# Cross-attention block: Q, K, V and the output projection by seven blocks, softmax weights left undivided, and a new order of all engines

## The chip, the cores and the metric

One core of one Trainium2 chip. The metric is device time in microseconds (us) for one launch of the kernel; of several runs the median is given. The engines are PE (TensorE, with PEld its weight loads), DVE (VectorE), ACT (ScalarE), POOL (GpSimd) and SP (SyncE, which here only issues transfers).

## The reference

128 batches of 128 tokens of 256 features, all in float32. Queries come from `x`, keys and values from `ctx_1024`; there are 16 heads of 16 features, and a token may attend only to the tokens ahead of it.

```python
q = (query @ Wq + bq)...; k = (key @ Wk + bk)...; v = (values @ Wv + bv)...   # 16 heads of 16
scores = einsum('bhqd,bhkd->bhqk', q, k) / 4
scores = where(j < i, scores, -1e30)
attn = softmax(scores, axis=-1);  attn[:, :, 0, :] = 0
attn_out = einsum('bhqk,bhkd->bhqd', attn, v)... @ Wo + bo
x = layer_norm(query + attn_out, ln1_g, ln1_b)
out = layer_norm(x + (relu(x @ W1 + b1) @ W2 + b2), ln2_g, ln2_b)      # W1: 256 x 1024
```

## The kernel before, in words

Batches go in pairs: there are NP = 64 pairs, and a pair has TP = 256 tokens. `KC` = 2 counts the 128-wide halves of the 256 features, `FC` = 8 those of the 1024 hidden ones. Nothing schedules the work: each engine runs its instructions in the order in which the code issues them (a manual schedule), and waits by semaphores where it needs another engine.

After a start written out by hand (`third` to `sixth`), the function `step(p)` (L1475) runs for p = 7 to 63, and a tail follows. One step does one part each for several pairs: the scores, exponentials and turning of pair p; queries and keys of pair p + 1 and values of pair p; the weighing of the values, the output projection and the first norm's statistics of pair p - 2; the first feed-forward product of pair p - 3; the second of pair p - 4; the second norm and the store of pair p - 5.

PE in a step: `weigh` (L544, L554) multiplies the turned softmax weights `pT` with the values in blocks of 32 columns. `scores_both` (L410) fills banks 0 to 3 with the scores of each batch's later 64 queries ("high", 128 keys) and banks 4 to 7 with those of the earlier 64 ("low", 64 keys). Then come queries and keys (`project`, L270), the output projection (`attention_out`, L573) and the values (`values`, L325): each is four matmuls of 128 x 128 weights with 256 moving columns. The two feed-forward products (`second_by_seven`, L878, and `Hidden.run`, L990) already go by seven block products in place of eight: 28 matmuls of 128 columns each, over sums and differences of blocks that POOL makes (`combine_hidden`, L859 to L862, and `combine_normed`, L952 to L955, with `w1t` and `wt` made once). Between the matmuls of L878 stand empty PE instructions (L219). The seven products lie in banks of their own, and DVE adds them up from there (L903, L919 and L926; L1002 to L1016).

DVE masks the high scores in their banks (L820) and takes maxima (L823); the low scores go to SBUF with their mask (L426, L434) and then get their maximum (L829). ACT takes the exponentials head by head with the row sum as a second output (L839). POOL then divides the weights by the row sums (`inverse` and `divide`, L480 and L485: three instructions of 1024 elements). DVE turns them in 32 x 32 blocks (`turn`, L497), and 16 transfers within SBUF put the blocks in place (`bring`, L512). ACT copies the weighed values (`context`, L566, tile `cxT`), the queries (L296), the keys twice, each time with half of the features set to zero (L315), and the values in two layouts (L340 `vz`, L349 `vd`), and does the relu (L1021) and both norms' scaling (L625, L662). POOL also adds the output bias to `x` (L263), makes the norms' scale and shift (L593, L594, L648), the residual (L637, L640) and the second norm's gain and bias (L672, L676). The normed tokens are turned by DVE (L742) and go through DRAM by four writes and one read (L246, L251).

Softmax weights, the turned blocks and `pT` of all pairs share four wide buffers (`wide`).

## Time and profile before

| | before |
|---|---|
| runs | 1483.75, 1484.87, 1485.62 us; median 1484.87 us |
| profiled execution | span 1482.7 us from its first to its last instruction; its own time is not given apart, the median of the runs is 2.2 us more |
| busy share of the span | PE 99%, PEld 93%, DVE 93%, ACT 89%, POOL 93% |
| granted TensorE clock | 0.999 |
| DMA | 204.63 MB, mean 138 GB/s |

How to read it: a share of busy time says how full an engine is, not how long it is waited for. PE's matmuls overlap, so the time of one is read from start to start, or from a run of equal ones; the same holds for two neighbours on DVE or ACT, where the next one starts before the record of the last one ends. A row such as `707.05 0.42 DVE L820 ...` gives start, duration, engine, line and operation, then output and inputs with their shapes; in square brackets stands the idle time ahead of it, and who ended it.

### The profile page before, as it was taken

Reading aid. Unit: us, or ns where it says so; the run is one execution under the profiler, and the core shown is the slowest. Engines: PE = TensorE matmul, PEld = TensorE weight load, DVE = VectorE, ACT = ScalarE, POOL = GpSimd, SP = SyncE. Lnnn points to the kernel's source line nnn. Section 1 sums busy time; section 2 is a strip of 40 time slices with the busy share of each in tenths; the row PEclk is TensorE's granted clock in tenths of the full one; section 3 lists DMA queues with packets and bytes.
Section 4 is the critical chain, followed back from the end, with each engine's and each line's share of the span. In section 5 each row is a group of like instructions: output and inputs, shape, how many; then the busy total and the mean of one; then the engine's idle time right before and its main releaser. Section 6 shows DMA issues by size and latency. Waiting matters only on the chain.

```text
span 1482.7 us, 53916 instructions
## 1 busy us (share of the span) xinstructions
PE 1475.0 (99%) x19367; PEld 1378.1 (93%) x19367; DVE 1386.3 (93%) x2444; ACT 1324.1 (89%) x5272; POOL 1376.5 (93%) x1530
## 2 busy tenths in 40 slices
PE   9999999999999999999999999999999999999998
PEld 7788999999999999999999999999999999999998
DVE  7999999999999999999999999999999999999977
ACT  6668999999999999999999999999999999999963
POOL 6979999999999999999999999999999999999987
PEclk9999999999999999999999999999999999999999
DMA  8366666555655566665556556566655666555451
GB/s 201 79 133 150 148 150 141 127 146 138 154 144 133 138 146 138 149 144 130 144 132 156 146 128 143 144 137 150 145 132 141 136 153 148 128 141 131 109 137 51
DMA packets 415317, 204.63 MB, mean 138 GB/s; under 512 B 282448, under 2 KB 383056, under 8 KB 415056
## 3 DMA queue, kind: packets, MB, share of 16 engines
q1 hardware_dynamic: 412768, 199.34, 57.5%
q8 instruction: 160, 2.62, 0.8%
q10 hardware_dynamic: 2288, 1.85, 0.5%
q14 instruction: 101, 0.83, 0.2%
HBM read 70.26 MB, written 33.29 MB: 70 GB/s over the span
## 4 chain that ended last, share of the span: by engine, by line
PE 96%; DVE 2%; POOL 1%; ACT 0%; issue 0%; DMA 0%; POOLq 0%; DVEq 0%
PE banks L878 25%; PE banks L990 25%; PE banks L270 15%; PE banks L573 7%; PE banks L325 7%; PE banks L410 6%; PE banks L554 4%; PE banks L544 2%; PE banks L778 2%; PE banks L1042 0%; PE banks L797 0%; DVE su L468 0%; POOL sm L446 0%; PE banks L527 0%; POOL sm L470 0%
## 5 line engine op out<-in xcount | busy, mean ns | idle before, releaser
L839 ACT ACTIVATE sm<-banks,nmx 128x128 f32<-128x128 f32 x944 | 329.8, 377 | 16.3 <-DVE nmx L823 8.7
L485 POOL TENSOR_TENSOR sm<-sm,rs 128x1024 f32<-128x1024 f32 x171 | 322.6, 1901 | 0.0
L839 ACT ACTIVATE sm<-sm,nmx 128x64 f32<-128x64 f32 x944 | 312.5, 368 | 0.0
L497 DVE STREAM_TRANSPOSE tb<-sm 128x1024 f32<-128x1024 f32 x186 | 229.8, 1237 | 17.1 <-DMA pT<-tb 6.9
L1021 ACT ACTIVATE hT<-hT,b1e_c 128x256 f32<-128x256 f32 x464 | 198.1, 497 | 34.7 <-DVE hT L1009 21.0
L839 ACT ACTIVATION_READ_ACCUMULATOR sm<-sm,nmx 128x1 f32 x912 | 201.6, 221 | 0.0
L839 ACT ACTIVATION_READ_ACCUMULATOR sm<-banks,nmx 128x1 f32 x912 | 197.3, 216 | 0.0
L990 PE MATMUL banks<-xS,w1t 128*128 128x128 f32 x1392 | 174.4, 275 | 0.0
L878 PE MATMUL banks<-wt,hS 128*128 128x128 f32 x1440 | 170.7, 275 | 0.0
L878 PEld LDWEIGHTS banks<-wt,hS 128*128 128x128 f32 x1440 | 165.6, 192 | 0.1
L990 PEld LDWEIGHTS banks<-xS,w1t 128*128 128x128 f32 x1392 | 164.8, 192 | 0.0
L823 DVE TENSOR_REDUCE nmx<-banks 128x4 f32<-128x512 f32 x177 | 153.9, 869 | 6.0
L270 PE MATMUL banks<-xT,wq 128*128 128x256 f32 x504 | 125.4, 392 | 0.0
L315 ACT ACTIVATE kT<-banks,bkh,half 128x256 f32<-128x256 f32 x252 | 122.5, 590 | 2.8 <-PE banks L270 2.8
L990 PE MATMUL banks<-x1T,w 128*128 128x128 f32 x944 | 124.6, 275 | 0.2 <-DMA x1T<-x1t 0.2
L573 PE MATMUL banks<-wo,cxT 128*128 128x256 f32 x512 | 121.2, 379 | 0.0
L325 PE MATMUL banks<-wv,cT 128*128 128x256 f32 x512 | 121.0, 379 | 0.0
L270 PE MATMUL banks<-cT,wk 128*128 128x256 f32 x504 | 119.4, 380 | 0.1
L878 PEld LDWEIGHTS banks<-w,hT 128*128 128x128 f32 x944 | 114.7, 192 | 3.1
L990 PEld LDWEIGHTS banks<-x1T,w 128*128 128x128 f32 x944 | 114.9, 192 | 0.4 <-issue 0.3
L878 PE MATMUL banks<-w,hT 128*128 128x128 f32 x944 | 115.2, 275 | 0.0
L573 PEld LDWEIGHTS banks<-wo,cxT 128*128 128x128 f32 x512 | 97.0, 190 | 13.5 <-ACT cxT L566 0.3
(191 smaller groups left out, 3954.1 us busy)
## 6 DMA issues: line engine op xcount, KB each, us to landing
pT<-tb SPq DMA_DIRECT2D x976, 96.0 KB, 2.2
x1t<-tbx SPq DMA_DIRECT2D x252, 64.0 KB, 2.4
x1T<-x1t SPq DMA_DIRECT2D x63, 256.0 KB, 3.0
out_dram<-t SPq DMA_DIRECT2D x63, 256.0 KB, 3.1
xb<-in_x_dram SPq DMA_DIRECT2D x124, 128.0 KB, 3.7
cb<-in_ctx_dram SPq DMA_DIRECT2D x124, 128.0 KB, 4.2
x<-in_x_dram SPq DMA_DIRECT2D x31, 512.0 KB, 5.3
w<-in_L_xattn_W_dram SPq DMA_DIRECT2D x2, 1024.0 KB, 8.3
```

Of the source, the lines that this page charges most:

```text
L270: nc.tensor.matmul(ps[:, m * TP : (m + 1) * TP], w[:, k, m * P : (m + 1) * P], src[:, k, :], start=(k == 0), stop=(k == KC - 1),)
L315: nc.scalar.activation(st["kT"][:, m, e, :], pk[:, m * TP : (m + 1) * TP], AF.Identity, bias=bkh[:, m, e : e + 1], scale=half[:, e : e + 1],)
L325: nc.tensor.matmul(pv[:, s * D : (s + 1) * D], st["cT"][:, k, s * P : (s + 1) * P], wv[:, k, :], start=(k == 0), stop=(k == KC - 1),)
L410: nc.tensor.matmul(st["sps", hi][r][s * HP : (s + 1) * HP, m * 2 * n : (m + 1) * 2 * n].rearrange("p (e j) -> p e j", e=2), st["qT"][strip ...
L485: nc.gpsimd.tensor_tensor(sm[:, part, :], sm[:, part, :], st["rs", hi][:, part, None].to_broadcast([P, part.stop - part.start, sm.shape[2] ...
L497: nc.vector.transpose(st["tb"][:, :, at : at + 256].rearrange("p j (n a) -> p n j a", a=32), st["sm", hi].rearrange("p h j -> p (h j)")[:, ...
L573: nc.tensor.matmul(po[:, s * D : (s + 1) * D], cxT[:, k, s, :], wo[:, k, :], start=(k == 0), stop=(k == KC - 1),)
L823: nc.vector.tensor_reduce(st["nmx", 1][:, 4 * first : 4 * (first + n)], ps, AX.X, ALU.max, negate=True,)
L839: nc.scalar.activation(sm[:, h, :], src, AF.Exp, bias=nmx[:, h : h + 1], scale=1.0, **({"accum_out": st["su", hi][:, h : h + 1]} if summed ...
L878: nc.tensor.matmul(out, left(k), right(k), start=(k == 0), stop=(k == FC // 2 - 1))
L990: nc.tensor.matmul(ps[:, i * P : (i + 1) * P].rearrange("p (n a) -> p n a", a=32), left(i), right, start=True, stop=True,)
L1021: nc.scalar.activation(self.hT[:, f], self.plains.get(f, self.hT[:, f]), AF.Relu, bias=b1e_c[:, f : f + 1], scale=1.0,)
```

## The change

Four things change, from p = 7 on.

*Products.* Queries, keys, values and output projection go by seven block products too (class `Seven`). The seven are not kept apart: they run as chains that add up in three 128-column parts of one PSUM bank. Part 0 takes product 1, then 6, 7 and 4 on top; part 1 takes 2 alone; part 2 takes 5, then 3. After 1, after 6 and after 7 ACT or DVE takes what part 0 holds so far, and only then may PE add the next product; after 4 the last reader takes it. The second feed-forward product (`Second`) gets the same form, and so does the first (`First`, with three whole banks as its parts). POOL makes the sums of blocks of `xT`, `cT` and `cxT` (four instructions of 128 columns each), and once those of the four weights. ACT writes the keys once, and then spreads them into two halves, one by ACT and one by POOL. The empty PE instructions are gone from the steps.

*Undivided weights.* POOL's `divide` goes. DVE inverts the 32 row sums of a row at once and turns them (`inverse`); they go to DRAM and are read back spread over the partitions (`send_inverse`, `fetch_inverse`); DVE multiplies them in where ACT copied the weighed values (`context`).

*Transfers.* The 16 moves of `bring` become four writes to DRAM and one read (`send_weights`, `fetch_weights`); the read of pair p - 1 stands in the middle of step p. Softmax weights, turned blocks and `pT` have one buffer each in place of four shared ones. The inverses take four small writes and two reads.

*Order.* `step(p)` walks a list of 150-odd short names. Each stands for one small piece of work; a suffix -1 or -2 means that it belongs to a step one or two earlier. The last pair has a function of its own (`last_step`), in the old order.

```diff
+    def inverse(p):
+        rs = small.tile([P, 2 * H], F32, tag="rs", name=f"rs_{p}")
+        rt = st["rt"] = small.tile([P, 32], F32, tag="rt", name=f"rt_{p}")
+        nc.vector.reciprocal(rs, st.pop("su"))
+        nc.vector.transpose(rt, rs)
...
+    def fetch_inverse(p):
...
+            nc.sync.dma_start(
+                inv[:, m].rearrange("p l s q -> p (l s q)"),
+                mid[m][:, None, :].to_broadcast([HH, DK, TP]),
+            )
...
     def context(p):
+        if "inv" in states[p]:
...
+                nc.vector.tensor_tensor(
+                    cxT[:, :, :, at], pc[:, :, :, at], inv[:, :, l, :, 1 - l :], ALU.mult
+                )
+            return
...
+    class Seven:
...
+            self.factors = {
+                1: (data(0, 0), weights(0, 0)), 2: (data(0, 1), weights(1, 0)),
+                5: (sums(0), mixed(0)), 6: (sums(1), mixed(1)), 3: (sums(3), weights(1, 1)),
+                7: (sums(2), mixed(2)), 4: (data(1, 1), mixed(3)),
+            }
...
+        def run(self, *which):
+            for n in which:
+                out = self.of({2: 1, 5: 2, 3: 2}.get(n, 0))
+                left, right = self.factors[n]
...
+                    nc.tensor.matmul(
+                        out, left(k) if self.depth > 1 else left,
+                        right(k) if self.depth > 1 else right,
+                        start=(n == 1 and k == 0), stop=(k == self.depth - 1),
+                        skip_group_check=True,
+                    )
...
+    class Onto(Seven):
...
+        def keep(self):
+            self.join(self.t[:, ::3], self.two(0, 2), self.base[:, ::3])
+        def keep2(self):
+            self.join(self.t[:, 1], self.a, self.base[:, 1])
+        def add(self):
+            self.join(self.t[:, 3], self.a, self.t[:, 3])
+        def add2(self):
+            self.join(self.t[:, :2], self.two(1), self.t[:, :2])
+        def rest(self):
+            self.join(self.t[:, 2], self.a, self.base[:, 2])
...
+    def combine_one(p, which, data, n):
...
+        left, right, how = {
+            0: (data(1, 0), data(1, 1), ALU.add), 1: (c[:, 0], data(0, 0), ALU.subtract),
+            3: (data(0, 1), c[:, 1], ALU.subtract), 2: (data(0, 0), data(1, 0), ALU.subtract),
+        }[n]
+        nc.gpsimd.tensor_tensor(c[:, n], left, right, how)
...
+    def send_weights(p):
...
+        for i in range(NS):
+            nc.sync.dma_start(mid[i].rearrange("j b n -> b j n"), tb[32 * i : 32 * i + 32])
+    def fetch_weights(p):
...
+        nc.sync.dma_start(pT, st.pop("ptd").rearrange("i j b n -> (j b) i n"))
...
+    ORDER = """
+        weigh re1-1 finish2-2 re2-1 re3-1 vr-1 hf-1 norm2-1 context scores hs2 store-2 ro2-1
...
     def step(p):
...
+        for key in ORDER:
+            key, late = (key.split("-") + ["0"])[:2]
+            q = p - int(late)
+            if FIRST <= q < NP - 1:
+                OPS[key](q)
```

What this moves on three engines is shown by pieces of the engines' orders. First PE, behind the scores of a step. Before, the four products stand one after the other (`xT` and `cT` are the turned inputs, `cxT` the weighed values, `w_139` is W2):

```order
L410 MATMUL banks<-kT_6672,qT_6652 64x128 x6
L270 MATMUL banks<-xT_6696,wq 128x256 [waits DVE_49]
L270 MATMUL banks<-xT_6696,wq 128x256 x3
L573 MATMUL banks<-wo,cxT 128x256 [waits DVE_49]
L573 MATMUL banks<-wo,cxT 128x256 x3
L270 MATMUL banks<-cT_6698,wk 128x256 [waits DVE_49,Activation_49]
L270 MATMUL banks<-cT_6698,wk 128x256 x3
L325 MATMUL banks<-wv,cT_6341 128x256 [waits DVE_49,Activation_49]
L325 MATMUL banks<-wv,cT_6341 128x256 x3
```

Now pieces of all six products alternate (`cc`, `oc`, `xc`, `hS` are the sums of blocks, `wvt`, `wot`, `wqt` those of the weights):

```order
L409 MATMUL banks<-kT_7132,qT_7043 64x128 x6
L1146 MATMUL banks<-wv,cT_7048 128x128 [waits DVE_49]
L1146 MATMUL banks<-wv,cT_7048 128x128
L1146 MATMUL banks<-wvt,cc_7105 128x128
L1146 MATMUL banks<-wo,cxT 128x128 [waits DVE_49]
L1146 MATMUL banks<-wo,cxT 128x128
L1146 MATMUL banks<-wot,oc_7358 128x128 [waits Pool_49]
L1146 MATMUL banks<-w_138,hT 128x128 [waits DVE_49]
L1146 MATMUL banks<-w_138,hT 128x128 x3
L1146 MATMUL banks<-wvt,cc_7105 128x128 [waits Activation_49]
L1146 MATMUL banks<-wv,cc_7105 128x128
```

The long runs of 256 columns are gone, and the second piece of a product waits for the engine that reads the first.

Second DVE, at the high scores of a step (`nmx` are the maxima, `t_23` the sum of attention and input). Before:

```order
L820 TENSOR_TENSOR banks<-banks,neg 128x4x64 [waits PE_49]
L823 TENSOR_REDUCE nmx_25_8694<-banks 128x4 [waits DVE_49]
L820 TENSOR_TENSOR banks<-banks,neg 128x4x64 [waits PE_49]
L823 TENSOR_REDUCE nmx_25_8694<-banks 128x4 [waits DVE_49]
L820 TENSOR_TENSOR banks<-banks,neg 128x8x64 [waits PE_49]
L823 TENSOR_REDUCE nmx_25_8694<-banks 128x8 [waits DVE_49]
```

Now (`t_25` and `t_23` are sums onto which the pieces of the output projection and of the second feed-forward product go):

```order
L1855 TENSOR_TENSOR banks<-banks,neg 128x4x64 [waits Activation_49]
L1855 TENSOR_TENSOR banks<-banks,neg 128x4x64
L1861 TENSOR_REDUCE nmx_27_9491<-banks 128x4 [waits DVE_49]
L1855 TENSOR_TENSOR banks<-banks,neg 128x4x64
L1298 TENSOR_TENSOR t_25_9545<-banks,x_8977 128x2x128 [waits PE_49,Pool_49]
L1855 TENSOR_TENSOR banks<-banks,neg 128x4x64
L258 STREAM_TRANSPOSE cT_9581<-cb_9353 128x512 [waits DMAHW5_49,DMAHW6_49,DMAHW4_49,DMAHW3_49]
L1861 TENSOR_REDUCE nmx_27_9491<-banks 128x4 [waits DVE_49]
```

Masking and maximum of one bank no longer stand side by side; other work lies between them.

Third POOL, in the middle of a step. Before, behind the sums for the first feed-forward product, two of the three divisions and the first norm's scale and shift:

```order
L955 TENSOR_TENSOR xS_10513<-x1T_10373,xS_10513 128x128 [waits Pool_49]
L485 TENSOR_TENSOR sm_10473<-sm_10473,rs_30_10600 128x1024 [waits DVE_49]
L485 TENSOR_TENSOR sm_10473<-sm_10473,rs_30_10600 128x1024 [waits Activation_49]
L593 TENSOR_SCALAR ve_28_10604<-mv_28_10580 128x2
L594 TENSOR_TENSOR sd_28_10605<-ve_28_10604,power 128x2 [waits Pool_49]
```

Now, sums of blocks of the weighed values (`oc`), the hidden tile (`hS`), the normed tokens (`xS`) and the turned context (`cc`):

```order
L1837 TENSOR_TENSOR oc_9530<-oc_9530,cxT 128x128 [waits Pool_49]
L1837 TENSOR_TENSOR oc_9530<-cxT 128x128
L1837 TENSOR_TENSOR oc_9530<-cxT,oc_9530 128x128 [waits Pool_49]
L1850 TENSOR_TENSOR hS_9524<-hS_9524,hT 128x512
L1850 TENSOR_TENSOR hS_9524<-hT,hS_9524 128x512 [waits Pool_49]
L1945 TENSOR_TENSOR xS_9629<-x1T_9560 128x128 [waits DMAHW4_49,PE_49]
L1837 TENSOR_TENSOR cc_9638<-cT_9581 128x128 [waits DVE_49,PE_49]
```

The 1024-element divisions are gone from POOL, and the instructions of 128 columns have taken their place.

692 lines of the change are left out of this document (553 added, 139 removed).

## The prediction, made before the run

> **What bounds the kernel now.** I read the page first, for the share of each engine and the chain that ended last.
>
> ```profile
> span 1482.7 us, 53916 instructions
> PE 1475.0 (99%) x19367; PEld 1378.1 (93%) x19367; DVE 1386.3 (93%) x2444; ACT 1324.1 (89%) x5272; POOL 1376.5 (93%) x1530
> ```
>
> TensorE (PE) is busy 99% of the span, but three other engines are at 89 to 93%: what PE gives back can be used only as far as they allow. So I look next at one repetition of the steady part, in which every engine does the same work once for each pair of batches: the chain that ended last, in order of time (start, duration, what), from one weighing of the values to the next.
>
> ```profile
> 704.16 0.36 PE banks L544 x16
> ...
> 705.64 1.55 PE banks L410 x45
> 707.19 1.92 PE banks L270 x8
> ...
> 712.57 1.73 PE banks L325 x8
> 714.29 6.25 PE banks L878 x56
> 720.55 6.25 PE banks L990 x56
> 726.80 0.36 PE banks L544 x16
> ```
>
> The whole chain of this stretch is PE. A step takes 726.80 - 704.16 = **22.64 us**; the change reaches 56 steps (p = 7 to 62), so 0.01 us of a step is worth 0.56 us. PE never stops: 1.48 for weighing the values, 1.55 for the scores, 7.10 (707.19 to 714.29) for Q, Wo, K and V, twice 6.25 for the two feed-forward products, which go by seven blocks already. One matmul of the program is two records here: a record of 256 columns takes 1.73 / 8 = 0.216 us, one of 128 columns 6.25 / 56 = 0.1116. The first group has 0.19 more (1.92 against 1.73), a gap behind the scores.
>
> **PE, part by part.** Sixteen matmuls of 256 columns become 28 of 128, so 32 records become 56: 56 x 0.1116 = 6.25 in place of 7.10. If the gap behind the scores stays, the step is 22.64 - 0.66 = **21.98 us**; if it goes too, 21.79. The two feed-forward products keep their 56 records each; the pads among those of L878 go, worth nothing, since 56 records with pads take the same 6.25 as 56 without (L990). That is 56 x 0.66 = 37 us at most, 48 with the gap. What is late next?
>
> **DVE.** The timeline of the same step, with slots from start to next start:
>
> ```profile
> 706.38 0.75 DVE L434 TENSOR_TENSOR sm<-banks,neg 128x256 f32<-128x256 f32 x2
> 707.05 0.42 DVE L820 TENSOR_TENSOR banks<-banks,neg 128x256 f32<-128x256 f32 x1
> 707.51 0.69 DVE L823 TENSOR_REDUCE nmx<-banks 128x4 f32<-128x512 f32 x1
> ...
> 722.46 0.69 DVE L1002 TENSOR_TENSOR hT<-hT,banks 128x512 f32<-128x512 f32 x1 [0.15 <-ACT hT L999]
> 723.26 0.69 DVE L1005 TENSOR_TENSOR hT<-hT,banks 128x512 f32<-128x512 f32 x1
> 724.16 0.69 DVE L1006 TENSOR_TENSOR hT<-hT,banks 128x512 f32<-128x512 f32 x1 [0.20 <-PE banks L990]
> 724.76 0.71 DVE L742 STREAM_TRANSPOSE tbx<-x 128x512 f32<-128x512 f32 x1
> ```
>
> Two independent instructions of 256 elements take 0.67 together, 0.335 each; one of 512 takes 0.60 (724.16 to 724.76). So an element costs 1.04 ns and an instruction 0.07 us on top. The maximum L823, which needs the sum L820 just ahead of it, starts 0.46 after it instead of 0.335: 0.125 for leaning on one's forerunner. The waits shown are 0.35, so DVE is occupied 22.29 of 22.64.
>
> The order of the change has 54 DVE instructions in a step where there were 38, over nearly the same elements (16.5 thousand against 16.7, summed over the free sizes). That is +16 x 0.07 = +1.12 and -0.2. It has four instructions directly behind the one that they need, where there were 14 (add and maximum are pulled apart, and the four sums L919 and L926 on one tile are gone): -10 x 0.125 = -1.25. Sum: 22.29 + 1.12 - 0.2 - 1.25 = **21.96**, level with PE. The weak number is the cost of 128 elements, which 14 of the new instructions have and no row shows. It lies between the 0.07 of an empty instruction and the 0.335 of 256; the slope gives 0.20, and I take that. At the lower end DVE would be at 20.1, at the upper at 23.9.
>
> [...]
>
> **POOL.** Again with slots:
>
> ```profile
> 708.28 1.27 POOL L859 TENSOR_TENSOR hS<-hT 128x512 f32<-128x512 f32 x1 [0.36 <-ACT hT L1021]
> ...
> 713.32 0.47 POOL L952 TENSOR_TENSOR xS<-x1T 128x128 f32<-128x128 f32 x1
> 713.73 0.47 POOL L953 TENSOR_TENSOR xS<-x1T 128x128 f32<-128x128 f32 x1
> ...
> 715.10 3.75 POOL L485 TENSOR_TENSOR sm<-sm,rs 128x1024 f32<-128x1024 f32 x2
> 718.95 0.23 POOL L593 TENSOR_SCALAR ve<-mv 128x2 f32<-128x2 f32 x1
> 719.25 0.71 POOL L594 TENSOR_TENSOR sd<-ve,power 128x2 f32<-128x2 f32 x1
> ...
> 722.22 1.27 POOL L637 TENSOR_TENSOR x1b<-x,g_r 128x512 f32<-128x512 f32 x1
> ```
>
> It is occupied 22.64 - 0.36 = 22.28. Three divisions go (two from 715.10 to 718.95): -5.6. Eight small scale instructions (718.95 to 722.22, 3.27) become four: about 0.7 for the power and 0.3 for each of the others, 1.6, so -1.7. Twelve combinations of 128 columns come at 0.41 (713.32 to 713.73): +4.9; one product of 512 for K's second half at the 1.27 of the other instructions of that size: +1.3. Sum **21.2**. The reciprocals now go through DRAM and into the copy of the weighed values, a DVE product (counted above) in place of ACT's copy.
>
> **ACT.**
>
> ```profile
> 705.71 0.58 ACT L566 COPY cxT<-banks 128x508 f32<-128x508 f32 x1 [0.56 <-PE banks L554]
> 706.49 1.71 ACT L1021 ACTIVATE hT<-hT,b1e_c 128x256 f32<-128x256 f32 x4 [0.20 <-DVE hT L1016]
> ...
> 708.67 0.36 ACT L839 ACTIVATE sm<-banks,nmx 128x128 f32<-128x128 f32 x1
> 708.92 0.20 ACT L839 ACTIVATION_READ_ACCUMULATOR sm<-banks,nmx 128x1 f32 x1
> ...
> 720.00 1.96 ACT L315 ACTIVATE kT<-banks,bkh,half 128x256 f32<-128x256 f32 x4
> 721.80 0.63 ACT L999 COPY hT<-banks 128x512 f32<-128x512 f32 x1
> 722.26 0.70 ACT L340 COPY vz<-banks 128x256 f32<-128x256 f32 x2
> ```
>
> Occupied at most 22.64 - 0.56 - 0.20 = 21.9. K's four copies (1.80) become three of 128 at 0.25 (708.67 to 708.92) and one of 512 (0.46 to 0.90; I take 0.66): -0.4. The copy of the weighed values goes: -0.58. Two more copies of 512 come at 0.46: +0.9. One of eight relus goes to DVE: -0.4. Four copies of Q and V become six halves: +0.2. Sum at most **21.6**.
>
> **Transfers.** The weights' 16 moves within SBUF become four writes and one read, each way 1.5 MB (128 x 3072 elements of 4 bytes).
>
> ```profile
> GB/s 201 79 133 150 148 150 141 127 146 138 154 144 133 138 146 138 149 144 130 144 132 156 146 128 143 144 137 150 145 132 141 136 153 148 128 141 131 109 137 51
> ```
>
> ```profile
> x<-in_x_dram SPq DMA_DIRECT2D x31, 512.0 KB, 5.3
> ```
>
> The slices of the steady part run at 128 to 159 GB/s; at 141 a step moves 3.2 MB, and with 1.5 more in 22 us that is some 215 GB/s, near the 201 of the first slice. By the row of a load, the last here (KB each, median us to landing), 1.5 MB read at once lands within three times 5.3 = 16 us if nothing overlaps. In the new order the writes stand early in the step after the turning and the read in its middle; the weighing follows in the next step. I take the transfers as hidden; without that cover each us of lateness costs 56.
>
> **Sum.** PE 21.98, DVE 21.96, ACT 21.6 at most, POOL 21.2. Two engines are level and hand sums to and fro (a bank is added to only after ACT or DVE has read it; 33 PE rows wait in a step, 21 before), so I add 0.1, the size of the waits above that are for one neighbour's last instruction: 22.07. Steady part: 56 x (22.64 - 22.07) = 32 us. Ahead, POOL trades six divisions (about 11 us) for 24 combinations (about 10); at the end the work is the same but for three divisions. I take both as 0, give or take 4. From the profiled execution's span 1482.7 this gives 1451; the median shown, 1484.87, lies 2.2 us higher, and 1453 is the same sum there. I forecast **1452**. With no loss at all it is 1437 to 1448, with 0.3 of loss 1465.
>
> **Rivals.** (1) *DVE takes the bound over, below the old step.* For it: its sum equals PE's, and PE's chains wait for it, as well as the transposes. Against: DVE is occupied 98.5% now and still costs PE almost nothing. A step of 22.3 to 22.6 gives 1466 to 1483. (2) *The small DVE instructions make it slower.* Place: the 14 instructions of 128 elements that read PE's banks. At 0.20 each DVE is level; it passes 22.64, and the kernel turns slower, above 0.20 + 0.68 / 14 = 0.25 each. At 0.28 the step is 23.1 and the time 1484.9 + 56 x 0.44 = 1510; at the bound 0.335 it is 1553. For it: no row shows such an instruction. Against: the slope. [...] (3) *The read of the weights lands late.* At 1 us a step it costs 56 and ends at about 1508. For it: twice the bytes on the path. Against: about a whole step of distance. (4) *The blocks bring nothing*, since waits fill the 0.66 on PE: 1485.
>
> **Chances.** Forecast (1437 to 1466): 0.68. Rival 1: 0.16, nearly all of it faster. Rival 2: 0.09, rival 3: 0.04, rival 4: 0.03. About 0.2% (3 us) is what a measurement of this kernel can tell from no change. So faster 0.83, same 0.04, slower 0.13. The range runs from 1438 to 1478: the forecast and most of rival 1, with the slower cases left out.
>
> **What would show it.** Right: the interval from one weighing to the next near 22.0 to 22.1; 56 records at 0.11 for Q, K, V, Wo; PE at 99% and in most of the chain; DVE instructions of 128 elements about 0.2 apart; POOL and ACT with waits of 0.4 to 0.8 us a step. Wrong: gaps ahead of the added-on products that end with DVE (rival 1 or 2), or ahead of the weighing that end with a DMA (rival 3), or a lower granted clock.

## The result, and the profile after

| | before | after |
|---|---|---|
| median of the runs beside each other | 1484.7 us | 1689.1 us (1682.3 to 1690.5) |
| after / before | | 1.137, 95% interval 1.135 to 1.139 |
| span of the profiled execution | 1482.7 us | 1688.8 us |
| granted TensorE clock | 0.999 | 0.972 |

The change makes the kernel 204 us slower; the forecast was 33 us faster. (Times below are of fast executions; one slow one, 1720.5 us of the run with half of the moves by ACT, is left out.) The page of the changed kernel (busy time, share, instructions):

```profile
PE 1520.8 (90%) x20711; PEld 1435.0 (85%) x20711; DVE 1390.3 (82%) x3338; ACT 1322.0 (78%) x5445; POOL 1331.7 (79%) x1877
```

No engine is full any more: where PE stood at 99%, all five have 10% or more of the span idle, so no engine's own work fills the step. Either they wait for each other, or for something that is no engine. The interval from one weighing to the next can be read from PE's timeline (here the weighings of pairs 6 and 61, as counting them from the start gives):

```profile
168.08 0.43 PE L556 MATMUL banks<-pT,vd 128*32 128x64 f32 x16
...
1603.92 0.43 PE L556 MATMUL banks<-pT,vd 128*32 128x64 f32 x16
```

(1603.92 - 168.08) / 55 = **26.1 us a step** in place of 22.64, and the steps are uneven. The waits from 200 to 1590 us (waiting engine and line, who ended it, us in total, times, longest) name many pairs, with transfers among them at every place where one can be waited for:

```profile
ACT vz L2012 <- PE banks L1146: 119.0, 41, 7.4
...
PE banks L556 <- DMA pT<-ptd: 59.1, 41, 4.2
...
DVE cxT L582 <- DMA invb<-inv: 38.1, 29, 2.9
...
POOL x L264 <- DMA x<-in_x_dram: 32.8, 23, 1.8
DVE tb L509 <- DMA ptd<-tb: 29.9, 27, 2.2
...
DVE t L1298 <- DMA out_dram<-t: 21.5, 12, 2.5
...
POOL xS L1945 <- DMA x1T<-x1t: 19.2, 12, 2.4
```

Waits of one engine for another (the first row is the largest) pass on a delay. Six kinds of transfer are late that have in common only SP's queue and the DMA engines: the weights' read (`pT`), the inverses (`invb`), the tokens (`x`), the weights' writes (DVE may not turn the next ones into `tb` before they have read it), the store and the normed tokens. So the queue itself comes next. SP's timeline of one step (`SPq` marks an issue of SP; the second column is how long the issue took, not the transfer):

```profile
823.70 3.78 SPq L1924 DMA_DIRECT2D x1t<-tbx  x4
827.60 0.39 SPq L730 DMA_DIRECT2D out_dram<-t  x1
830.41 0.38 SPq L1929 DMA_DIRECT2D x1T<-x1t  x1
830.89 4.31 SPq L1954 DMA_DIRECT2D ptd<-tb  x4
835.24 4.53 SPq L490 DMA_DIRECT2D inv<-rt  x4
840.09 0.80 SPq L1961 DMA_DIRECT2D pT<-ptd  x1
841.98 1.32 SPq L498 DMA_DIRECT2D invb<-inv  x2
843.35 0.47 SPq L99 DMA_DIRECT2D x<-in_x_dram  x1
843.86 9.45 SPq L92 DMA_DIRECT2D xb<-in_x_dram  x4
853.42 2.02 SPq L1924 DMA_DIRECT2D x1t<-tbx  x4
855.57 1.50 SPq L730 DMA_DIRECT2D out_dram<-t  x1
857.96 0.38 SPq L1929 DMA_DIRECT2D x1T<-x1t  x1
858.77 4.21 SPq L1954 DMA_DIRECT2D ptd<-tb  x4
```

From one `ptd` to the next pass 858.77 - 830.89 = 27.9 us, 24.8 of them in SP's issues; of the other 3.1 it waits 1.7 until writes of its own have landed (ahead of `pT`, `invb` and `x1T`). This round of issues and landings is called the ring below. Three things are to be seen. The read `pT` needs the four writes `ptd` to have landed, and stands 9.2 us behind their first issue. Behind that read of 1.5 MB SP takes 9.45 us to issue four loads. In the run without the weights' transfers (below) the same four, also with the load `x` just ahead, take 5.31:

```profile
825.15 5.31 SPq L92 DMA_DIRECT2D xb<-in_x_dram  x4
```

Third, the writes of the normed tokens `x1t`, which DVE had turned by 845.3 (L1914, from 844.56, 0.70 long), are issued at 853.42; their read `x1T` waits until they have landed, and the next weights stand behind it.

### The profile page after: what moved, and what is told of

It is laid out like the page before. It is cut to its first block, busy times and chain, and to the rows that moved or that the text cites. A ratio compares the mean times of both kernels' runs of the same rounds, so it can differ in the third digit from the quotient of the medians.

```text
span 1688.8 us, 56436 instructions
## 1 busy us (share of the span) xinstructions
PE 1520.8 (90%) x20711; PEld 1435.0 (85%) x20711; DVE 1390.3 (82%) x3338; ACT 1322.0 (78%) x5445; POOL 1331.7 (79%) x1877
## 5 line engine op out<-in xcount | busy, mean ns | idle before, releaser
L891 ACT ACTIVATE sm<-banks,nmx 128x128 f32<-128x128 f32 x944 | 336.7, 368 | 47.4 <-DVE nmx L1861 41.3
L891 ACT ACTIVATE sm<-sm,nmx 128x64 f32<-128x64 f32 x944 | 320.5, 350 | 12.7 <-DVE nmx L880 12.7
L1850 POOL TENSOR_TENSOR hS<-hT 128x512 f32<-128x512 f32 x112 | 143.3, 1280 | 75.2 <-ACT hT L1392 66.8
L891 ACT ACTIVATION_READ_ACCUMULATOR sm<-banks,nmx 128x1 f32 x944 | 194.9, 206 | 0.0
L891 ACT ACTIVATION_READ_ACCUMULATOR sm<-sm,nmx 128x1 f32 x944 | 190.1, 201 | 0.0
L409 PE MATMUL banks<-kT,qT 32*64 32x128 f32 (+1 forms) x3840 | 129.4, 351 | 55.0 <-issue 48.6
L409 PEld LDWEIGHTS banks<-kT,qT 32*64 32x64 f32 x3840 | 91.0, 139 | 81.8 <-issue 57.5
L1146 PE MATMUL banks<-w,hT 128*128 128x128 f32 x896 | 124.5, 284 | 1.2 <-issue 1.2
L2012 ACT COPY vz<-banks 128x128 f32<-128x128 f32 x56 | 14.9, 266 | 136.6 <-PE banks L1146 121.9
L556 PE MATMUL banks<-pT,vd 128*32 128x64 f32 x2048 | 56.8, 226 | 66.7 <-DMA pT<-ptd 59.1
L264 POOL TENSOR_TENSOR x<-x,bov_r 128x512 f32<-128x512 f32 x64 | 81.3, 1270 | 38.8 <-DMA x<-in_x_dram 38.8
L1837 POOL TENSOR_TENSOR oc<-cxT 128x128 f32<-128x128 f32 x112 | 51.2, 457 | 73.2 <-DVE cxT L582 72.7
L1392 ACT ACTIVATE hT<-hT,b1e_c 128x256 f32<-128x256 f32 x224 | 108.1, 509 | 0.7
```

Of the source, the lines that this page charges most:

```text
L264: nc.gpsimd.tensor_tensor(xb, xb, bov_r[:, None, :].to_broadcast([P, 2, D]), ALU.add)
L409: nc.tensor.matmul(st["sps", hi][r][s * HP : (s + 1) * HP, m * 2 * n : (m + 1) * 2 * n].rearrange("p (e j) -> p e j", e=2), st["qT"][strip ...
L556: nc.tensor.matmul(pc[32 * j : 32 * j + 32, at : at + HP], st["vd"][:, s, 4 * m + j].rearrange("p e d -> p (e d)"), pT[:, 2 * s : 2 * s + ...
L891: nc.scalar.activation(sm[:, h, :], src, AF.Exp, bias=nmx[:, h : h + 1], scale=1.0, **({"accum_out": st["su"][:, at : at + 1]} if summed e ...
L1146: nc.tensor.matmul(out, left(k) if self.depth > 1 else left, right(k) if self.depth > 1 else right, start=(n == 1 and k == 0), stop=(k == ...
L1392: nc.scalar.activation(self.hT[:, f, at], self.hT[:, f, at] if src is None else src, AF.Relu, bias=b1e_c[:, f : f + 1], scale=1.0,)
```

## The experiments

All ratios are to the kernel before, run on the same chip. Theory A said that the transfers hold the step; theory B, the first rival, that the chained products, the hand-overs and the new order do. A had to be split later.

### Is it the products or the transfers?

**The weights not moved** (leaves out their moving from p = 7 on; every weighing uses the weights of pair 6):

```diff
     def send_weights(p):
+        if p > FIRST - 1:
+            return
...
     def fetch_weights(p):
+        if p > FIRST - 1:
+            st["pT"] = kept["pT"]
+            return
```

> The changed kernel without moving the weights: from p = 7 on neither the four writes nor the read are issued, and every weighing uses the turned weights of pair 6 (it leaves out the moving of the weights, all engines' work stays). Theory A: nothing of 343 - 172 = 171 engine-us a step can hold an engine up, so the step is the 21.98 to 22.3 us of the prediction's sum, the time 1450 to 1470 us. Theory B: at least 25 us a step, above 1610 us.

Measured 1477.8 us, ratio 0.996 (0.994 to 0.997). Theory B falls: with all products, hand-overs and the new order, all of the 204 us are gone and 6 more (1483.9 us beside it). (The expectation's engine-us are the time of the 16 DMA engines in the traces: for the changed kernel 0.82 x 16 x 26.1 = 342 a step (share from 400 to 1530 us), of it 1024 packets of 3 KB for the weights, which took 169 ns in the mean.) The time is some 8 us above A's range (taken up below, with the steps of the prediction). Its page shows the engines full again:

```profile
PE 1461.0 (99%) x20711; PEld 1398.9 (95%) x20711; DVE 1382.0 (94%) x3338; ACT 1310.8 (89%) x5445; POOL 1328.8 (90%) x1877
```

**All transfers, but 1/32 of the weights' bytes** (leaves out the moving of the rest):

```diff
+            n = slice(0, 24 if p > 6 else (H + HH) * 32)
-            nc.sync.dma_start(mid[i].rearrange("j b n -> b j n"), tb[32 * i : 32 * i + 32])
+            nc.sync.dma_start(
+                mid[i].rearrange("j b n -> b j n")[:, :, n], tb[32 * i : 32 * i + 32, :, n]
+            )
...
```

and the read likewise.

> The changed kernel with all of its transfers, but of the weights only 24 of the 768 columns of each block are moved (it leaves out the moving of the rest; the weighing uses the weights of pair 6 for them). The number of transfers and of packets and every wait stay, the bytes fall by 31 of 32 parts for the weights. If it is the time that the weights' bytes take until they land, for which SP waits in order: 22.2 to 22.8 us a step, 1475 to 1510 us. If it is the number of issues on SP alone: as the changed kernel, above 1600 us.

Measured 1477.0 us, ratio 0.995 (0.993 to 0.997). The number of issues and of packets (461858, as in the changed kernel) costs nothing; the bytes do.

**The detour alone, in the kernel before:**

```diff
-        bring(p, nc.sync, LATE_FIRST[: len(EVERY) // (1 + last)])
+        for i in range(NS):
+            nc.sync.dma_start(mid[i].rearrange("j b n -> b j n"), st["tb"][32 * i : 32 * i + 32])
+        nc.sync.dma_start(pT, mid.rearrange("i j b n -> (j b) i n"))
```

> The kernel before with one thing changed: its 16 moves within SBUF become four writes to DRAM and one read behind them, at the same place at the end of a step. Theory A, if the sum of the traffic decides: 219 - 101 + 172 = 290 engine-us are 18.1 of 22.64 us, which still fits, and the distance to the weighing is a whole step, so the time stays within 1483 to 1510 us. If instead the waiting of SP on its own writes decides (the read stands behind them, the loads of the next step behind the read), the loads land late and the time is 1520 to 1600 us. Theory B: 1485 us, the detour costs nothing.

Measured 1572.1 us, ratio 1.059 (1.057 to 1.062): the second case. With none of the new products the way through DRAM costs 88 us by itself. SP's timeline has the same ring, 24.2 us from `ptd` to `ptd`:

```profile
819.48 4.40 SPq L521 DMA_DIRECT2D ptd<-tb  x4
828.83 0.38 SPq L524 DMA_DIRECT2D pT<-ptd  x1
...
843.65 4.83 SPq L521 DMA_DIRECT2D ptd<-tb  x4
```

**The detour undone, the rest of the change kept** (the 16 moves stand where the four writes stood; that edit of the order is not shown):

```diff
-        "fetchp": lambda p: fetch_weights(p - 1),
+        "fetchp": lambda p: bring(p - 1, nc.sync, LATE_FIRST),
```

> The changed kernel with one thing undone: the weights go by the 16 moves within SBUF of the kernel before, all issued by SP at the place of the four writes; products, order and inverses stay. Theory A (the transfers are the bound: in the changed kernel they keep the 16 DMA engines busy for some 343 engine-us a step, 172 of it for the weights; 16 moves need about 101): about 272 engine-us are 17 of 22 us, so the step falls from 26.3 to 22.1 to 23.2 us and the time to 1455 to 1515 us. Theory B (the chained products and the new order lose the time, by hand-overs between PE, DVE and ACT): the step stays above 25.5 us, the time above 1640 us.

Measured 1684.0 us, ratio 1.136 (1.134 to 1.138): this run speaks against A as it stood. (The 101 engine-us of the expectation are 512 packets of 3 KB a step, which took 197 ns in the mean in the kernel before.) The bytes through DRAM are gone and nothing is won. In the stretch from 400 to 1300 us (busy us of PE, PEld, DVE, ACT, POOL, then clock, DMA share, GB/s) the changed kernel and this run read

```profile
400.00:1300.00 900.00, 803.00 (x11336) 767.07 (x11325) 743.65 (x1853) 728.09 (x3080) 712.30 (x1028) 0.97 0.81 192
```

```profile
400.00:1300.00 900.00, 808.26 (x11387) 780.93 (x11376) 743.61 (x1864) 730.74 (x3106) 716.08 (x1037) 0.96 0.60 134
```

The DMA engines are busy 0.81 in one and 0.60 in the other, and the time is the same. So A was split: A1, SP's one queue, served in order; A2, the time of the DMA engines.

### The DMA engines' time, or the landing in SP's order?

**The bytes put back where nobody waits for them** (leaves out the moving, as above):

```diff
     def send_weights(p):
         if p > FIRST - 1:
+            nc.sync.dma_start(kept["spare"][0], kept["ptd"])
             return
```

and the same with a second copy in place of the read.

> The run without any moving of the weights (1478 us; it leaves out that moving) with as many bytes put back in which nobody is interested: SP issues, at the places of the four writes and of the read, one copy each of 1.5 MB from DRAM to DRAM, in packets of 3 KB as many as the weights have; nothing waits for them. If the time of the DMA engines decides (the other transfers land late behind these bytes): 1600 us or more, near the changed kernel. If it is the waiting for the weights' own landing: 1478 to 1510 us.

Measured 1479.2 us, ratio 0.997 (0.995 to 0.998). The same stretch as above:

```profile
400.00:1300.00 900.00, 897.95 (x13183) 874.85 (x13182) 867.25 (x2180) 847.70 (x3635) 836.35 (x1213) 1.00 0.81 227
```

The DMA engines are as busy as in the changed kernel, and PE does not notice (busy 897.95 us here, 897.60 without the copies). (SP does wait, ahead of `invb` for the inverses' writes that stand behind a copy, 208.6 us in 49 times from 400 to 1300 us; in this ring it has the room.) So A2 falls, with one reserve: the packets were not of 3 KB, as the expectation says; the page counts 405408 packets for 310.82 MB, against 400031 for 134.64 without the copies, so these are some 33 KB each. As many bytes in fine packets with nobody waiting were not tried; this run and the one with 1/32 of the bytes say that neither the bytes (without waits) nor the packets (with few bytes) cost anything alone. The last run below settles the reserve.

**No transfers of the inverses** (leaves out their moving; the weights go through DRAM as in the change):

```diff
     def send_inverse(p):
+        if p > 6:
+            st.pop("rt")
+            return
...
```

and the reads likewise, with the inverses of pair 6 in their place.

> The changed kernel without moving the inverse row sums: from p = 7 on neither their four writes nor their two reads are issued, and the copy of the weighed values multiplies by the inverses of pair 6 (it leaves out the moving of the inverses; the weights still go through DRAM). Theory A: the inverses are a small part of the bytes but some 2000 packets of 128 bytes at 19 ns, about 40 engine-us a step, and six of SP's transfers in its one queue; the step falls by 1.5 to 3 us to 23.3 to 24.8, the time to 1520 to 1605 us. Theory B: no change, above 1670 us.

Measured 1543.0 us, ratio 1.040 (1.034 to 1.046), in the range of A: 146 us for six transfers with few bytes. (Packets of 128 bytes took 18.4 ns in the mean in the trace of the changed kernel, near the 19 of the expectation, but they are not 2000 a step: over the whole run that trace has 7552 of them and 15104 of 1 KB more than the kernel before.) That range was set down before A was split and names both the packets and SP's queue, so it does not part A1 from A2. **One write of the inverses in place of four:**

```diff
-        for b in range(NS):
-            nc.sync.dma_start(mid[:, b], rt[32 * b : 32 * b + 32])
+        nc.sync.dma_start(mid.rearrange("i b r -> b i r"), st.pop("rt"))
```

> The changed kernel with the inverses written by one transfer in place of four; bytes, packets and order stay. Leaving out all six transfers of the inverses had brought 146 us. Theory A1: three issues fewer on SP, and each of the transfers behind them waits for one that is three further back: 40 to 100 us less, 1590 to 1650 us. Theory A2: nothing is taken from the DMA engines, so 1680 us or more.

Measured 1672.1 us, ratio 1.126 (1.124 to 1.129). Only 17 us, between the two forecasts. By the rows of the changed kernel the four issues (835.24 to 839.77) lie in the time in which SP waits for `ptd` to land (840.09), so that fewer of them gain little there.

**The 16 moves again, in another order on SP.** The lines of this diff, and of the later ones that begin like it, are not code: they list what SP issues in a step. `sendx` and `readx` are the writes and the read of the normed tokens, `sendp` and `fetchp` those of the weights, `sendi` and `fetchi` those of the inverses; `loadx` is the load `x`, `load` the four loads.

```diff
-        store, readx, 16 moves, sendi, fetchi, loadx, load, sendx
+        3 moves, readx, store, 13 moves, sendi, loadx, load, fetchi, sendx
```

> As the run with 16 moves on SP, but in SP's new order: three moves, the read of the normed tokens, the store, 13 moves, the writes of the inverses, the loads, the read of the inverses. SP issues some 12 us of moves and 9 of the rest in a step of 22, with one landing to wait for. Theory A1: 22.5 to 24 us a step, 1480 to 1560 us, above the run with two queues. Theory A2: as before the new order, 1684 us.

Measured 1548.0 us, ratio 1.043 (1.041 to 1.045), in A1's range. **And with the inverses earlier and in one write:**

```diff
+        store, 3 moves, readx, sendi (one write), 13 moves, loadx, load, fetchi, sendx
```

> As the run with 16 moves on SP in its new order, with two changes: the inverses are written by one transfer in place of four, and right behind the third move, so that 13 moves and the loads cover their landing; their reads stand last. Theory A1 (SP issues in order, and an issue waits until the transfer eight before it has landed): SP issues 21 transfers in some 18.5 us of a 22.2 us step and waits for nothing long; the step is 22.2 to 22.6 us, the time 1470 to 1500 us, at best level with the kernel before or 1% under it. Theory A2 (the 16 DMA engines' time): the bytes are those of the run before, so 1540 us or more.

Measured 1509.9 us, ratio 1.018 (1.017 to 1.019), 10 us above the range. From 1684 to 1510 nothing but the order on SP and three small writes has changed. So the moves are no way out by themselves: SP needs 11 to 12 us to issue them (11.15 in the kernel before, 11.98 in the run of 1684 us), and in the changed order everything else stood behind. This is the best of the changed kernels here that compute the whole of it; it is still 1.8% slower than the kernel before.

### Ways round the queue that failed

**The weights issued by ACT:**

```diff
-            nc.sync.dma_start(mid[i].rearrange("j b n -> b j n"), tb[32 * i : 32 * i + 32])
+        nc.scalar.dma_start(mid[i].rearrange("j b n -> b j n"), tb[32 * i : 32 * i + 32])
```

one at a time between exponentials, and the read likewise.

> The changed kernel with the weights' four writes and their read issued by ACT in place of SP, one at a time between exponentials; bytes and packets are the same. Theory A1 (SP's one queue, served in order, is the bound: what it issues, what it waits for until transfers land, and what stands behind): SP is rid of about 5 us of issuing and of the wait for the writes, so the step falls from 26.3 to 22.5 to 24 us, the time to 1480 to 1560 us; ACT has 1.2 us a step to spare, so some of its five issues must be hidden behind its instructions. Theory A2 (the time of the 16 DMA engines is the bound, 21.4 us of work a step in gusts): no change worth speaking of, above 1650 us.

Measured 1767.3 us, ratio 1.191 (1.187 to 1.195): outside A1's range, and no "no change" as A2 said, but 78 us more. The waits from 400 to 1300 us say why:

```profile
ACT sm L891 <- DMA invb<-inv: 127.4, 32, 5.8
```

ACT waits ahead of an exponential for a transfer of SP that neither the exponential nor the write of the weights uses. The listing of this program gives its 1404 transfers eight semaphores in turn, whichever engine issues them, and each of ACT's 224 writes of the weights waits there for the transfer that last had its semaphore. One of them, for which the turned tile had long been there:

```
L1953 DMA ptd_13172<-tb_12978 32x4x768 [waits DMAHW5_49]
```

So an issue on ACT drags ACT into SP's queue. **The copies that nobody waits for, issued by ACT:**

```diff
-            nc.sync.dma_start(kept["spare"][0], kept["ptd"])
+            nc.scalar.dma_start(kept["spare"][0], kept["ptd"])
```

> The same two copies of 1.5 MB, issued by ACT in place of SP. If the DMA engines' time decides: as with SP. If SP's order decides (its small transfers queue behind the copies): 1478 to 1500 us here, and more with SP.

Measured 1584.5 us, ratio 1.068 (1.064 to 1.071): slower than with SP, against both. The same kind of wait (`ACT sm L891 <- DMA inv<-rt`, 83.1 us in 35 times) is the largest in it. **Half of the moves by ACT, one at a time, with SP's new order:**

```diff
+        OPS[f"m{n}"] = lambda p, n=n: bring(p - 1, nc.scalar, LATE_FIRST[8 + n : 9 + n])
```

> The changed kernel with the 16 moves within SBUF in place of the way through DRAM, eight issued by SP and eight by ACT, one at a time between exponentials, and with SP's new order. Theory A1: SP has 6 us of moves in place of 12 and waits for no weights, so about 15 of 22 us; the step is the 22.2 to 22.5 us of the run without any moving, the time 1465 to 1490 us. If ACT can't hide issues of 0.6 us (its tail before shows 6.38 us for eight in a row), ACT needs 21 + 4.8 us and the step is above 25 us, the time above 1610 us. Theory A2: the 16 engines have 17 us of work as in the run with 16 moves on SP, which took 1684 us; this run should then take the same.

Measured 1695.2 us, ratio 1.141 (1.139 to 1.144), where A1 forecast 1465 to 1490; above 1610 was forecast for an ACT that can't hide its issues. These take it some 0.5 us each, but ACT again stands still ahead of an issue: in one step its second move goes out at 808.65 and its third at 812.72, with a wait of 2.56 us ahead of the exponential behind it. (The row names DVE as the one who ended it; that the shared semaphores hold the issue is taken over from the first of these runs, and not shown here.)

**The writes of the weights first on SP, the reads last:**

```diff
-        store, readx, sendp, sendi, fetchp, fetchi, loadx, load, sendx
+        sendp, readx, store, sendi, loadx, load, fetchp, fetchi, sendx
```

> The changed kernel with SP's transfers in another order and nothing else: the four writes of the weights first, then the read of the normed tokens, the store, the four writes of the inverses, the loads of the tokens, and only then the two reads of weights and inverses, so that something is issued while the writes land. Theory A1: two of the three landings that SP waits for are covered by issues, some 2 us each, and the step falls to 22.8 to 24.5 us, the time to 1495 to 1590 us. Theory A2: bytes and packets are the same, so above 1650 us.

Measured 1730.6 us, ratio 1.166 (1.163 to 1.168), outside A1's range and above 1650, as A2 said. The covered landings were paid for by others that now lie behind 1.5 MB:

```profile
DVE t L1298 <- DMA out_dram<-t: 106.0, 33, 4.1
...
POOL xS L1945 <- DMA x1T<-x1t: 39.7, 33, 2.1
```

**Inverses and loads ahead of the normed tokens' read and the weights** (the store in fact stayed first):

```diff
+        store, sendi, loadx, load, readx, sendp, fetchp, fetchi, sendx
```

> The changed kernel with one move in SP's order: the writes of the inverses and the loads of the tokens come ahead of the store, the read of the normed tokens and the writes of the weights, in place of behind the reads. Theory A1: the loads no longer stand behind the read of 1.5 MB and the inverses no longer behind the writes of 1.5 MB, but the reads of weights and inverses now follow the weights' writes with nothing between: 1580 to 1690 us. Theory A2: above 1670 us.

Measured 1755.9 us, ratio 1.183 (1.181 to 1.185), outside A1's range and above 1670, as A2 said. By their numbers these two orders speak for A2; their waits show a late landing in another place: here the normed tokens became the ones that are late (`POOL xS L1945 <- DMA x1T<-x1t`, 111.4 us in 30 times).

**DVE turns the high parts later,** in the changed kernel and in the run of 1510 us:

```diff
-        turn1 h5 eh0 kk2 w4 hk2 res0 turn0 el2 k3 h7 hk5 res1 ka kb norm1 h2 qa vb ha xc1
+        h5 eh0 kk2 w4 hk2 res0 el2 k3 h7 hk5 res1 ka kb turn1 norm1 h2 qa vb ha turn0 xc1
```

> The changed kernel, weights through DRAM, with DVE's two high turnings behind six of its sums in place of ahead of them, so that the writes of the weights have 2 to 3 us more. If the single turned tile (written again while its writes still stand in the queue) were what holds the changed kernel: some 1 to 2 us a step less, 1580 to 1640 us. If it is the transfers' time and SP's order: 1670 us or more.

> As the run of 1510 us (16 moves on SP, early and single write of the inverses), with one change: DVE turns the two high parts behind six of its sums in place of ahead of them, some 2 to 3 us later in the step. In the run of 1510 us DVE waited 61 us in all ahead of the turning, for moves that still read the one turned tile. Theory A1: those waits go and the step is 22.2 to 22.5 us, the time 1470 to 1495 us. Theory A2 (the DMA engines' time): the bytes stay, 1505 us or more.

Measured 1686.0 us (ratio 1.136, 1.134 to 1.138) and 1598.5 us (ratio 1.077, 1.075 to 1.078). In the changed kernel the single turned tile is not the bound. In the other the forecast was wrong by 100 us. (Of the 61 us that its expectation puts down to the moves 18.6 end with a move; 21.2 end with ACT's `kr`.)

```profile
DVE kr L1225 <- PE banks L1144: 98.0, 37, 2.7
```

The two turnings had filled the time in which PE makes K's pieces. Put behind, DVE waits 2.65 us a step for them (98.0 / 37) and then has the turnings on top.

### The ring cut at one place

**The loads ahead of the two reads, all else as in the change:**

```diff
-        store, readx, sendp, sendi, fetchp, fetchi, loadx, load, sendx
+        store, readx, sendp, sendi, loadx, load, fetchp, fetchi, sendx
```

> The changed kernel with one move in SP's order: the loads of the tokens (four or five) come between the writes of the inverses and the read of the weights, in place of behind the two reads; all else stays, the weights go through DRAM, all bytes and packets too. Theory A1, as it now stands: the 26 us are one ring on SP, read from the trace of the changed kernel: writes of the weights until they have landed 8.6 us, their read until it has landed 6.6 (the loads stand behind it, since an issue waits for the transfer eight before it), the loads 6.6, the normed tokens' writes and the wait for them 4.5. With the loads ahead of the read they fill the time in which the writes land, and the ring loses up to 6.6 us: SP is no longer the bound, the step is 22.2 to 23.2 us, the time 1478 to 1535 us. If it is DMA time after all (no ring): 1680 us or more.

Measured 1598.0 us, ratio 1.078 (1.076 to 1.081): 91 us less by one move of four or five issues, though 63 us short of the range. (Of the reason in the expectation one part is wrong: in the changed kernel no semaphore makes the loads wait for the read; SP takes longer to issue them shortly behind the read, 9.45 us above against 5.31 in the run without the weights' transfers.) SP's timeline:

```profile
830.59 4.55 SPq L1954 DMA_DIRECT2D ptd<-tb  x4
835.18 4.24 SPq L490 DMA_DIRECT2D inv<-rt  x4
839.47 1.30 SPq L99 DMA_DIRECT2D x<-in_x_dram  x1
840.81 3.99 SPq L92 DMA_DIRECT2D xb<-in_x_dram  x4
844.90 0.78 SPq L1961 DMA_DIRECT2D pT<-ptd  x1
...
848.85 1.30 SPq L1924 DMA_DIRECT2D x1t<-tbx  x3
```

The loads take 5.3 us in place of 9.9, and `x1t` follows 4.0 us behind the read, where it was 13.3. But in the steps with the extra load `x` the read is issued 14.3 us behind the first write. **That load in the other steps, and one write of the inverses:**

```diff
-        sendi, loadx-2, load-1
+        sendi (one write), loadx-1, load-1
```

> The run before it (loads ahead of the reads, 1598 us) with two edits that its trace asks for. In every second step a load of 512 KB comes on top of the four of 128 KB, the read of the weights is issued some 5 us later than in the step before, and the weighing waits for it (60.9 us in 19 waits): that load goes to the other steps. And SP stands 4.2 us at the four writes of the inverses, of which the last wait for transfers eight before them: they become one write. Weights still go through DRAM, bytes and packets stay. Theory A1: the read is issued by 17 us after the weighing in every step and lands ahead of the next; the step is 22.2 to 22.8 us, the time 1478 to 1515 us, at best 0.4% under the kernel before. Theory A2: no change, 1598 us.

Measured 1538.7 us, ratio 1.037 (1.035 to 1.038): another 59 us, 24 above the range. The stretch from 400 to 1300 us reads

```profile
400.00:1300.00 900.00, 861.41 (x12695) 837.18 (x12694) 831.74 (x2077) 810.75 (x3458) 798.85 (x1152) 0.99 0.83 216
```

The weights go through DRAM in the same fine packets (310.82 MB in 458316), the DMA engines are busy 0.83 where it was 0.81, and the kernel is 150 us faster than the changed one by its order and three small writes fewer. So it was not the DMA engines' time. What is left is shown by SP's and PE's rows:

```profile
822.18 4.36 SPq L1952 DMA_DIRECT2D ptd<-tb  x4
...
834.65 0.81 SPq L1959 DMA_DIRECT2D pT<-ptd  x1
```

```profile
819.76 0.43 PE L554 MATMUL banks<-pT,vd 128*32 128x64 f32 x16 [0.91 <-DMA pT<-ptd]
...
843.64 0.43 PE L554 MATMUL banks<-pT,vd 128*32 128x64 f32 x16 [0.66 <-DMA pT<-ptd]
```

2.4 us from the weighing to the first write, 12.5 until the read is issued, 9.0 until the next weighing can start: 23.9 us, and the weighing waits for the read at both ends. There is one `pT`, so the read may not begin before the weighing ahead of it; and DVE completes the turned tile only then (its last turning runs from 818.75 to 819.98), so the writes may not begin before it either. Here the way through DRAM fills the whole step; of the 39 weighings from 400 to 1300 us 18 wait for the read, 25.0 us in all. A second `pT` or `tb` was not tried.

## Why the prediction was wrong, step by step

- **"I take the transfers as hidden": the step that failed.** The sum put the transfers at nothing, and they cost 211 us, the changed kernel against the run without the weights' transfers. Rival 3 named the mechanism (the read lands late), at 1 us a step and a chance of 0.04; it was 3.7 us a step (26.1 against 22.4 below), since one late read makes the loads, the normed tokens, the store and the next writes late, all in the same queue. "About a whole step of distance" left out two things that the order on record shows: the 9.2 us until the writes have landed come ahead of the read, and SP reaches the writes only after it has waited for `x1t` to land, to issue `x1T`. My own bound was 16 us for the read alone; with the writes ahead of it that is more than a step. The bandwidth, which I did work out (215 GB/s), is not what failed: the run with the spare bytes moved 227. (The slices that it reads as 128 to 159 GB/s are 127 to 156 up to 1370 us; the mean of 141, which it uses, is not touched.)
- **PE 21.98.** Near, by a run without the weights' transfers: 0.40 of the 0.66 a step came. Its timeline:

```profile
816.33 0.43 PE L556 MATMUL banks<-pT,vd 128*32 128x64 f32 x16
...
817.86 1.82 PE L409 MATMUL banks<-kT,qT 32*64 32x128 f32 x64
819.61 0.71 PE L1146 MATMUL banks<-wv,cT 128*128 128x128 f32 x4
...
838.57 0.43 PE L556 MATMUL banks<-pT,vd 128*32 128x64 f32 x16
```

  The interval is 838.57 - 816.33 = 22.24. The scores with the gap behind them take 1.75 (1.55 + 0.19 was forecast), the 168 records of the six products 18.96, where 168 x 0.1116 = 18.75. So the gap stayed, as forecast, and 0.21 is lost among the pieces; the weighing takes 0.05 more (1.53 against 1.48).
- **"I add 0.1" for handing sums to and fro.** Mis-sized: 0.21 in a smooth step. Over the whole of it, with the weighings of pairs 5 and 61 before, and of 5, 6 and 61 in the run without the transfers,

```profile
138.21 0.43 PE L544 MATMUL banks<-pT,vd 128*32 128x64 f32 x16
...
1405.78 0.43 PE L544 MATMUL banks<-pT,vd 128*32 128x64 f32 x16
```

```profile
139.92 0.43 PE L556 MATMUL banks<-pT,vd 128*32 128x64 f32 x16
...
167.20 0.43 PE L556 MATMUL banks<-pT,vd 128*32 128x64 f32 x16
...
1397.13 0.43 PE L556 MATMUL banks<-pT,vd 128*32 128x64 f32 x16
```

  55 steps take (1397.13 - 167.20) / 55 = 22.36, not 22.07: 16 us more than forecast; most take 22.23 or 22.24, single ones up to 23.34. The first step of the new order takes 27.28, which I had not seen at all: 5 us. The stretch ahead is 1.7 us longer (139.92 against 138.21) and the one behind 2.8 (1476.8 - 1397.13 against 1482.7 - 1405.78), within the 4 allowed. These 26 us are the difference between 1452 and 1478: without the weights' transfers the change would have brought 6 to 7 us, not 33.
- **DVE 21.96, with 128 elements at 0.20.** Right in size; rival 2 falls. Starts 0.19 and 0.23 apart, in the same run:

```profile
812.74 0.28 DVE L1187 SCALAR_TENSOR_TENSOR qT<-banks,qT 128x128 f32<-128x128 f32 x1
812.93 0.28 DVE L1272 TENSOR_TENSOR vz<-banks,vz 128x128 f32<-128x128 f32 x1
813.16 0.69 DVE L1382 TENSOR_TENSOR hT<-banks,hT 128x512 f32<-128x512 f32 x1
```

- **Rival 1** (DVE takes the bound over, 22.3 to 22.6 a step, 1466 to 1483 us) has the numbers of that run, 22.36 and 1477.8. Its cause does not show. The waits from 400 to 1300 us, some 40 steps, have DVE waiting for PE,

```profile
DVE t L1298 <- PE banks L1146: 13.3, 43, 0.4
DVE kr L1227 <- PE banks L1146: 11.7, 40, 0.3
```

  and PE for DVE 1.7 us in all, its weight loads included. With two smaller rows DVE waits 26.9 us, 0.67 a step, so that it is occupied some 21.7 of 22.36. Losses of PE in smaller pieces are not in that list, and what makes the 0.21 stays open.
- **ACT and POOL** have room in that run (89% and 90% busy), as forecast. Rival 4 (1485 us, the blocks bring nothing) is 6 to 7 us off there.
- **A lower granted clock**, which I had named as a sign of being wrong, came too (0.972; 0.999 without the weights' transfers). It goes with most of the waits, but not with all: the run of 1598.5 us has 0.997. Its price is not shown apart. PE runs the same 20711 records in both and is busy 1520.8 us with the waits against 1461.0 without, 60 us more; the clocks would make an estimated 41 of it (1461.0 x 0.999 / 0.972). But the two largest groups of records (1344 each) have nearly the same mean in both runs, 277 and 275 ns against 275 and 275. Part of the 60 is in the counting: a record of 128 columns takes 0.1116 us in a run of equal ones, while the last one ahead of a gap counts with its whole 0.275. How the 60 divide stays open.

## What to carry to other kernels

A queue whose transfers are issued in order by one engine is to be counted like an engine: add up what it issues in a step (24.8 of the 27.9 us of the pass shown), and at each read of something just written put the landing of the write into the sum (9.2 us there from the first write to the read), before any bandwidth. A transfer with one buffer at either end has only the time between two uses of these buffers, and a round trip through DRAM has to fit the landing of its writes and that of its read into it (in the last run 12.5 us until the read is issued and 9.0 until the weighing can start, of 23.9). Before such transfers are made, take them out in an experiment: the 6 to 7 us that the change brings without them were the most that could be won in this order.

## What the runs showed of the hardware that was not expected

- From 700 to 1000 us four loads of 128 KB took SP 9.3 to 11.3 us to issue in the changed kernel, with the read of 1.5 MB shortly ahead, and 4.4 to 5.7 in the run without the weights' transfers, both with the load `x` between; in the steps without `x` 6.7 to 8.5 against 2.9 to 4.1. The listing of the changed kernel has no semaphore ahead of these loads, so it is the issue itself that takes longer, and SP is held up with it. Why it takes longer is not shown.
- Spreading transfers over two issuing engines made it slower three times (1767, 1585 and 1695 us, against 1689, 1479 and 1548 with SP alone). In the first of the three ACT waited up to 5.8 us for SP's transfers.
- Two copies of 1.5 MB a step that nobody waited for, 227 GB/s in all, made the kernel 1.4 us slower (1479.2 against 1477.8), within the intervals.
